# A four-layer hybrid on one core: new ranks for the written-out order, and slot counts in tiles of 96, 112, 104 and 128 rows

## The chip, the core and the metric

The kernel runs on one core of one Trainium2 chip. The metric is the device time of one execution in microseconds (us); the median over runs is what two kernels are compared by. The engines are named as in the profile: PE is the matrix engine (PEld its weight loads), DVE the vector engine, ACT the scalar engine, POOL the engine that also issues indirect DMAs, SP the queue that issues most plain DMAs.

## What is computed

The input x is 16 sequences of 256 tokens with 128 features. Four layers follow each other, each as x = x + layer(layernorm(x)):

```python
x = x + attn_a(layernorm(x))   # softmax over an axis that the einsum then sums out: it comes to x @ (w_v, w_out)
x = x + ffn(layernorm(x))      # 8 experts, each token goes to its best 2, weights by softmax of the two
x = x + attn_b(layernorm(x))   # a selective scan with 16 states per feature, along 256 tokens
x = x + ffn(layernorm(x))      # the same experts again
```

The experts have 128 inputs, 512 hidden units with relu and 128 outputs, all in float32.

## The kernel before, in words

**Blocks and sets.** The 4096 tokens lie in 8 blocks of 512 tokens (2 sequences). For the first expert layer the blocks are grouped into the sets `FIRST = ([0], [1], [2, 3], [4, 5], [6, 7])`, for the second into `SECOND = ([0, 1], [2, 3], [4, 5], [6], [7])`. In a set, each of the 8 experts has a fixed number of slots. `SLOTS` gives that number by layer and by the number of blocks in the set: 192 for one block and 330 for two in the first layer, 216 for one and 384 for two in the second. `divided` cuts the slots into equal tiles of at most 128 rows: 192 = 2 x 96, 330 = 3 x 110, 216 = 2 x 108, 384 = 3 x 128. If an expert draws more tokens than it has slots, a flag is set, and at the end a general kernel computes everything again.

**The stages of one block.** `attention` loads the block (`xT`), transposes it to token rows (`x`), and adds the first layer. `gate` normalises (`xn`), transposes (`xnT`) and multiplies by the gate matrix (`lg`). `route` picks two experts per token and numbers the slots (`to`, `of`), scales the rows (`row`) and scatters them with 8 indirect DMAs per block on POOL into `slots` in DRAM. `experts` takes one expert of a set after the other: a plain DMA on SP fetches its slots (`xs`), PE transposes them, a copy moves them to SBUF (`xsT`), PE makes the hidden units (`ps_b`, relu into `h` on ACT or DVE) and the outputs (`ps_y`, copied into `yT`), PE transposes back, a copy (`yr`) and a plain DMA write `ys` in DRAM. `collect` gathers a block's two results per token with 8 indirect DMAs on POOL (`yy`) and adds them to `x` on POOL or DVE. `mixer` is the selective scan: for each of 8 pairs of states ACT makes `decay` and `th`, PE broadcasts B and C (`ps_B`, `ps_C`, from `pieces` and `sel`), and DVE makes a product on `ps_B`, a scan into `w`, a product on `ps_C` and a product into `th`; two such `th` are added on POOL or DVE and PE sums the result into `ps_s`. At the end `sos` is transposed and added to `x`. `finish` gathers the second expert layer, transposes and stores (`out_T`).

**Who sets the order.** The program is first written down as a list of jobs (`Plan.job`); nothing is emitted then. Each job has one or more ways (engine, duration, call): copies, relus, products of two tensors and row scalings can go to either of two engines. Durations come from the functions `cost` (DVE, ACT, POOL) and `matmul` (PE). `Plan.order` decodes one rank per job from the string `ORDER` and plays the list through (`Plan.forward`): at each step it takes the ready job and engine with the earliest start, and of equal ones the best rank. The result fixes, for each engine, the order of its instructions, which engine does a job that has a choice, and which buffer a tile gets. On the chip each engine then works through its own list in that order, and an instruction that waits holds back all that stand behind it on its engine. So a rank or a duration in the table changes the order and the choice of engine, and no arithmetic.

In a mixer, the pairs are summed like this (`ADD` is 2, `NS` is 16):

```python
            group.append(th)
            if len(group) > 1:
                product(group[0], group[0], th, ALU.add)
            if len(group) == ADD:
                for k in range(2):
                    matmul(so, wsh_s, group[0][:, k, :], False, n + k == NS - 1)
                group = []
```

In the profile, nearly every instruction carries line 710 (the helper that makes the calls); scatters carry line 807 and gathers line 821. The tile names are what tells instructions apart.

Of the kernel before, what the change touches and what calls it, by code (L numbers as in the profile page):

```python
# [40 lines left out]
XN, ROW, XS, XT, H, YT, DEPTH = 4, 3, 4, 3, 4, 3, 3  # L41

ORDER = (
    "c-oy;3zS?{m92a3_kHWtzxw}AcS6!hI-~;z$O;57;6V8Q2_u0S5d^_uSc)<WMU9}iM3yW-9GO9x!6gH;R9KFnMgszpL;?f?f"
    "k*<R^Xq@t@4Y*x(n)u9Rdv$gbywAU_uY5jJ?HGR&pu3!7%XbbZAPKv1@3dL7-PWr9y>~ce89&%(C@K%Jo9!(hVu?i`7ck&TU"
    "=}!eF%Vl)_8eOGlzoV+GCP40*uyj))&`!j{^V`L0}L96gZ<4gs;O)2b>A*3(6>rA1qHftKE)g1PD&+d4C53zj>tYtuRmST4)"
    "&WZ=i;-Wdt8&k}Jkz4frZfW0dx>2F9<qDP7bBq>YMzaZlQu8;l;?+ePSH#x<oKoEc04YdQ9_z#2UcR8YkQZ@_JKUIwrXpCBw"
    "y%n$|z+H*Fet87`^C*_nH1fcC_oYqiEa5-i%s&Llw`v@46X#t7>ItB=v6B`tD>z8D<E*H}0f-#>loAIJY14hsV+|<5QxV>F6"
    ">MACb|KehA*xQaiirRK`r;~{cLjneDt0Nf|kEoo*U@p9_j!i#dWsezvrR+sxshv)zuWsGhFh-7pml~U+|6RMg#e{BnBi1OJ8"
    "{AtKz1A~GTIhQXQRn%ke_1+;3-()<bWZJRR6xkpvtH^UoJyCT1TFBd-vKZw{l=N5^8I7n;k;oMd;@Ct0ds)?$Q&UmPXz}F6#"  # L50
    "dW9?-*SWOvxor10@uUMTT|4)h($^?t#9+p%<8@UwC4u_H&;{uTgXsAMiMbl@4dSA0RXZ4ACKM^vhG!qIZ3nF^_^|>`d-Tn&K"
    "wyzk<LlLQRB1Sh~zY_bopU;AF}%AS(s#+{Wm8iwK;{49U2`nGz1AY|+UEUrmJ%G;LyF9NZ`WH88wyQ>luGWVmKT3OV<!#{EW"
    "z!NIr5>A!W@A}UR$AWI|yFk+BEncN=R!(&QNPwlz&?wY>(L5$Xj@WkfMZ5@g#l8cWfdX#yell3CZhJqETdv4Sl?uKS~-)v})"
    "*4Vd22ckBKk|8VVy=0BLVS=}uE1S@ZYfgCSgm>u8<lgqPqc<;kc?rNJurWMKMhvbR2qEm+|2UcJKs<96Vvpuj0d3D4Ol{~jD"
    "cbd9cbIWM858=Cz7YhCRBII%{;(YO>*0hKYgrutqLc+%P%RBi3%*?jzD0>I3<3Efd@<bwI+I<3KauaD-H2gE37^e)@TEs7Rl"
    "mCTe(M@e{Hq2=o>!CxJnq#en9mpN*lS+&Iw2j!+`ts4{f2PVMHH#yYYq^BZsi=|-|t8(JfC6;{iqKJpA{YQK>8{db}Y7%1%m"
    "$WPD1#pR5Rju3=MF*JyEdPx|=W?&I655)808;G9f7ezWWA3XfwvOg@aHMUvd&5l5TnkS>p^$u;L$4aYP5jbo}#ADG_H0DKuj"
    "u!Z7tjkurLfov96nM^nzTX@8{Q$937vRW0C-5uOb^Oj3%l#B4<#!j~c5E#e_fwC;J+RCpwK|NPft1JPleU~<FVRNIdf6eaz_"
    "Nv0P>Z+A!CEICH}&6*u~1??PyUf7eg8@uY%b;<r%k|>f-k1T$sZg1Me)YxXVdWNeW?%8tuHdp{3#ogBbYA;w0bivzZvubm=S"
    ";u|tWYNdXxF6B#=HHK)3%~O5?RK;+SsOX+qgTI%sagY#bZ33c{lh?fXeo(UeK9XlQ!l>}&R7jB33OpT{afUf*+^D_6L!6*c<"  # L60
    "h7L9m@!!-^s_fy|QfmDvDt?3h}Vp{*$OLDcCS%nsc8svmPfsu)&;TDFcKF;EU}a@<8*34~xXDg|A}%sHpKTeo9dE`>kiXNE!"
    "2}Rao~0CdHr>Vh5vv;!0oyH0!d8k45OvgXmyL7+J<Yl^FG(U|O>XL3Z^p+mWlK0Gj2vl>bFE98-Xh<|d<ttXm_ycw_46$d*="
    "N{H*TW<G$1MvHzy|X*oCAKl|_DUET4E2{EZ~6~SV(+hdkJ2eiw&E}+CZo)u}D7<-j8X)h}#*5`2TRY(d%ak`I(om3YX7XQ;-"
    "82r-(aOFxjFT(DFH3&d<{WUmyg<*(gK;*T8E51PH6`c5O%$++arQY0k=N}_YL3^ZMXC|Hk8Tkp7kug{EMoc)KVA>SNEd*jOR"
    "9YC!pixRCZz|TuC8>TjE2Sd2j>|k}_jex`*77FX%xVN5;iP64HL+aT94Q(>1jRGe9_6W#Uzmtbw}b7x^s&|tS_9HVKCt5A<r"
    ";K3#2~{Q$LJJ~Hs`_xjttq@*ZSwWyjf2SC@AZj@tRoMK)SD!2#kI>vgzGf`??{<_J?ayD>|GN-@g6sACYC`O>cGby6Yag{&{"
    "i}+$XP#SP|(-qF~Kw%fXLgv}ls@Vcf(y{7%z2MX{bU?!9o?c~7re&u%04nm5av&iTz*iXBTg#+qYc$6S5>Z_diGZg@Lf6Z@l"
    ")wW4G;Y_;oS5sUq}{^J@BankP?#tvB!n0-i|(&S41wf@8QeqzI@v|6^xKn>E_@SbQwN(5yWll87$l4ZQ+dV~^R$DnXlPzYRo"
    ")nh#23O4sr7AdIyNKVav-OU8V&iXsz8B^JL-v%twpAwQ=Qp|pL-T}0+fY4v3M`J_Ct2}NOAeM^U#$*H;)v^arT5v56Py~LZy"
    "KtG#Z#A8=wV{w6{Aq2UK4;F$;&&I4XD{lhb2fGEE&R*a#-{EVssn+QktixhOrgXABzgXo6auRe$x$=KXq4BsUH~Xp{8b1kln"  # L70
    "N+6lChLhmik8mt@M}Y;tMZR#K=n$X_u5IpFss8+P{mW+v!LiI0f_TD5d!MEHHWJ{fMhI2>AeM8WT~lFC&MDJMTtfyM<#FVQG"
    "6lvYlzEg5Xy?ijwILJC0%|7jEaAdM4HQ9Ul^>ZtxO2d*7_vQ`_~SaB^+CfzpN?51RLemBMwz*BO@dmSRRDbMiV)Q)90R8v)z"
    "PHZ9pW?~U#))Iqb7HGfO(OYbK0V2jtFoI3HtT9vb*jfliR`xD_|=fpUst#pJqUfuD|?7`1i9dy4PmcQ6C_ua2TI`NL#X@*mg"
    "FRefEuh)`e$Qz<7@yzC)%_k#wz7<VN(?nT?jN!h38#$$@B&A}fNhKD)_V3C>6?W_Km;UG4d2i226s4(^Prc~oj9DzqGETcK8"
    "l1I%Z`po^mmqr`!`l4Z+3U}RBpKnhl}a~$D~2#N!gR!o$meVKHLX;2^h2XY87cFhMkAv)*fxxquK9mk7i_+QICRJ`ksSbxqM"
    "*I8qi^KK9B8|S>`kad*b*wWhc}`O7B-;)d)e~yQKVGI!z@(HG(2T0$>Pb^WShXEOR;`2lv#Y9kQb>_Ogj2i=fq_yU67CeVZr"
    "{@gsGEVbJj_oU$d>DPTCh!;?-g}h~-P|d6M0v5E0K_4$xYQ1gxnot`W$KR~PH@`L`l|7UC;<sTQxWUQ6||poTy22!i!IhKzy"
    "pXQf3l-Gg!A-@Dv~rsY^rO)gVE@UZZmD)VdP0}msHuac5QY{JGYJL#qvpHEjmiedOSa1F&HY|ulVc)O@cHts`I{@eiBjwR(!"
    "_8ix^k!l0(h~&T7vM4e5KVN*DYOK3E+dhbWdb3?O^7)&A1eAW?=7Vz!2K8hi*_g1DL}BPd81oY)3j%rzwa6$#het4-Ihzya7"
    "77H$j6raj9Caxc6jsy)rla2BZ#kLR!ussM?-TivyE_K=-%6eQ%Dy}IKPmF8KGQE(BPY{&sD0aUkypJowK$5&pz3Zxld!;r4b"  # L80
    "i{@8#QJ_IFn*;{VzcdLVpURg@j=$V-dy;p8g9$&<0E*5r}RnW4ssP!0vkwhv!q5M?mqtJQ-&7z$ANdJr>3`CNU5J!(3K065A"
    "i+L-$}&JeEnTAef=kA}-sw&-e>J#HChX&52<yMomPBiDcydpfxkF<esn+mybj<nYg@AEfou;>8oatI$$gl&*zUTVA&_w=>d0"
    ")VuxalN-e>{1?hHd#T<gEY603Sq;ya#Gqh_Mm3NVtcv12paWEAp@N;jl_QKli;?LCjg<s`!{TB$IU6ISyA=LpWVI7x57}ZFu"
    "UyR@ii5A&vj>Y+kR=nMcOp1blceu7K&ZmLJKbnmXE#R8F_*sih9<z#X+;A%6{A{Ez$^$XzqzsgPamGSd;v$zQUxv|TBU}pJO"
    "amc?{~0On8j*%t>`(S5uz_(gF0ig2eO`~@C)l`YfsL7i$mXvUPy{QQMzyN>t{N*$*BV(<B)RH{Zi?qJ-47zZD6A6QTNl6PX5"
    "ISpC}NRp5Pnd{WL_F(JZ&*EA26kJwh%tbQBz`jL{MqK*a1OmW2Y&=;)dCIpY+M<9hn6WW0SGk%=for-_rsND|HXUrYeDY^Wt"
    "uRc9iXm1sqF%8mqwdiz%BgB3yFq0D1xK{)d$SD=|z!!`R#$kn*RmVr&^uNvVT^94rO$#9JszL!=M5ANyV03eex*#vqAJ5%Ny"
    "4jqAju=(&N=4uCL$VU#40LZNbPG?#1NILG;DwkqZqSz2uCi;rN@$1`Lu><|JJbQm8p-oY1<G0KV!2gME%*-8+W+2sVI7iO}V"
    "by#4#`*ZG+D5_>`9E(B_QH4OGPsRbTmB)28Dj{m%J|AhKbS}aVhfpCwQ3T%8MPLEt0_hZ!m=-&iwY`GPJ764^K~`KA)|>;ZT"
    "@}ro$BSFRTs>(OgIUG3@gF-FYys&tR|0K7L5=Q1R;Acpqk2X^1mlt)<4r;#9V#Ar;xBaY8bA8LwH`k|bnD=W9={Cqp~?6mho"  # L90
    "&4_Wy<Nnt3%6`4o`d?Jc7`~W)6IU(A0xWeYE66moHm&C{%Swf1)8>zM4L0V)e(guDC4q`lQj5u0A+aaZ8un3Qd1Ymv1sxdPR"
    "bXpF`2ny4=hvZmZ(jB1TFvQ!y*3d@871G&uZwjyQCLcvtak_0a06QK|H{u2@M=iF$eXLNf~A_>t8mIX5}CBwCXxTAHI}2I<h"
    "`E~}xkx}PS^I0)w{z$;7M(mMgE@bH1*P=z1LhC|cMJ}fL|GOVkadMHZ|Iwe#A`toNgp%6N%#M5OoJ7Xx|oBi^Al<r1{j)cBY"
    "l~?L1sL<2Fxe}N<G+K_!DGWB1<tAJ`9fwY^rJe?ox=L6Hjs_FgT9+F+bp=uascEUaWHugt_1Qsn0t`Y``6H-EgwhO|E(3LFi"
    "Z?4fSLUZ9QdC9!r$s_l{2aE7_!YHqVmIU{%F`z!%!=I%kKZ5%&Cmzc%b~}~q>IM!rb81tqy!K!VUCYqq#7$!!==bhCX=3s;$"
    "%^*;wCa3OO-O9o(ZQ-hqNQio)L;mia^O(WxDCmOmSION~THP!{KuJTjQtx^z2P$M2bgM$Pd4pP-rZqEAXmI7_yZA^bv5zLiv"
    "(<9@0~Uc6m5-C3WfQIGd(iPb1aJH#rlw)TN|RU9cU3796-NOrQ-8{Em$WuY$d&)W2z2U6(ZvewlXCrKM0GRTY^=ugp-!=%Y&"
    "Fsu8My`l0<!hGyKW_?@eYMLo3~SMyobTC68?dK%$h)m{3q^-@n)MyH}zA67bsj(WIKz)be3x{NFe<qcAG^{A`%9Fy8f&&*3R"
# [1408 lines left out]
```

## Time and profile before

| what | value |
|---|---|
| median of 9 runs | 724.24 us (721.89 to 728.17) |
| the profiled execution, its own time | 726.89 us |
| its span on the core | 725.2 us |
| PE busy | 626.5 us (86%) |
| DVE busy | 554.1 us (76%) |
| ACT busy | 487.5 us (67%) |
| POOL busy | 414.0 us (57%) |
| mean granted TensorE clock | 0.915 |

The shares are means over stages of different kind: the beginning, in which the first blocks are loaded and gated, the long middle, in which mixers of some blocks run beside experts of others, and the end, in which only experts are left. The span is the time between the first and the last instruction in the trace; the execution's own time is 1.7 us longer.

### The profile page before, as it was taken

Reading aid. Unit: us, or ns where it says so; the run is one execution under the profiler, and the core shown is the slowest. Engines: PE = TensorE matmul, PEld = TensorE weight load, DVE = VectorE, ACT = ScalarE, POOL = GpSimd, SP = SyncE. Lnnn points to the kernel's source line nnn. Section 1 sums busy time; section 2 is a strip of 40 time slices with the busy share of each in tenths; the row PEclk is TensorE's granted clock in tenths of the full one; section 3 lists DMA queues with packets and bytes.
Section 4 is the critical chain, followed back from the end, with each engine's and each line's share of the span. In section 5 each row is a group of like instructions: output and inputs, shape, how many; then the busy total and the mean of one; then the engine's idle time right before and its main releaser. Section 6 shows DMA issues by size and latency. Waiting matters only on the chain. (4 is left out here: it accounts for less than half of the span.)

```text
span 725.2 us, 8786 instructions
## 1 busy us (share of the span) xinstructions
PE 626.5 (86%) x2598; PEld 392.1 (54%) x2598; DVE 554.1 (76%) x1038; ACT 487.5 (67%) x996; POOL 414.0 (57%) x490
## 2 busy tenths in 40 slices
PE   5478999799999769899898889787999999999970
...
DVE  4765448999998898899999898998898998740120
...
GB/s 234 327 115 52 94 99 42 73 53 47 88 88 17 1 30 46 123 58 33 31 68 83 56 33 25 55 59 21 51 31 80 156 51 70 86 46 104 98 133 76
DMA packets 76373, 55.05 MB, mean 76 GB/s; under 512 B 8064, under 2 KB 69152, under 8 KB 76320
## 3 DMA queue, kind: packets, MB, share of 16 engines
...
q8 instruction: 22, 0.36, 0.2%
...
q14 instruction: 31, 0.25, 0.1%
...
## 5 line engine op out<-in xcount | busy, mean ns | idle before, releaser
L710 PE MATMUL ps_b<-xsT,w_s 128*128 128x330 f32 (+3 forms) x640 | 212.3, 441 | 15.3 <-ACT h L710 6.8
L710 PE MATMUL ps_y<-h,w_s 128*128 128x330 f32 (+3 forms) x640 | 213.9, 425 | 3.4 <-ACT yT L710 2.2
L821 POOL DMA_INDIRECT yy<-ys,of x128 | 124.6, 973 | 101.3 <-DMA ys<-yr 38.5
L807 POOL DMA_INDIRECT slots<-row,to x128 | 126.4, 987 | 79.3 <-issue 22.2
L710 ACT ACTIVATE h<-ps_b 128x384 f32<-128x384 f32 (+2 forms) x234 | 110.1, 475 | 90.0 <-PE ps_b L710 86.4
L710 PEld LDWEIGHTS ps_b<-xsT,w_s 128*128 128x128 f32 x640 | 115.9, 198 | 74.5 <-ACT h L710 24.4
L710 DVE TENSOR_TENSOR_SCAN w<-decay,ps_B 128x1024 f32<-128x1024 f32 x64 | 145.8, 2278 | 0.2
L710 PEld LDWEIGHTS ps_y<-h,w_s 128*128 128x128 f32 x640 | 109.9, 195 | 44.9 <-issue 11.8
L710 ACT ACTIVATE th<-later,lneps,ha_s 128x512 f32<-128x512 f32 x128 | 100.1, 809 | 5.1 <-DVE th L710 2.9
L710 ACT ACTIVATE decay<-delta,nea 128x510 f32<-128x510 f32 x128 | 86.6, 714 | 4.8 <-DVE w L710 3.5
L710 DVE TENSOR_TENSOR ps_B<-du,ps_B 128x1024 f32<-128x1024 f32 x64 | 78.2, 1221 | 13.3 <-PE ps_B L710 13.1
L710 DVE SCALAR_TENSOR_TENSOR ps_C<-th,ps_C 128x1024 f32<-128x1024 f32 x56 | 68.2, 1218 | 7.4 <-PE ps_C L710 7.3
L710 PE MATMUL ps_s<-th,wsh_s 128*128 128x512 f32 x128 | 69.6, 636 | 3.8 <-POOL th L710 3.8
L710 DVE TENSOR_TENSOR th<-ps_C,w 128x1024 f32<-128x1024 f32 x56 | 67.9, 1212 | 0.2
L710 POOL TENSOR_TENSOR th<-th,th 128x1024 f32<-128x1024 f32 x20 | 47.2, 2358 | 29.6 <-DVE th L710 27.2
L710 POOL TENSOR_TENSOR rstd<-var,root 128x8 f32<-128x8 f32 (+1 forms) x20 | 28.2, 1411 | 52.4 <-DVE var L710 49.7
L710 PEld LDWEIGHTS <-sel 96*128 96x128 bf16 x256 | 25.9, 103 | 59.0 <-issue 48.5
L710 PE MATMUL ps_B<-pieces,sel 96*128 96x512 bf16 x128 | 42.0, 402 | 10.3 <-DVE w L710 10.1
L710 PE MATMUL ps_b<-ident,yT 128*110 128x128 f32 (+3 forms) x208 | 43.6, 279 | 3.0 <-ACT h L710 1.5
L710 PE MATMUL ps_b<-ident,xs 110*128 110x110 f32 (+3 forms) x208 | 38.9, 278 | 7.2 <-ACT h L710 3.2
L710 PE MATMUL ps_C<-pieces,sel 96*128 96x512 bf16 x128 | 41.7, 406 | 3.1 <-DVE th L710 2.9
L710 PEld LDWEIGHTS ps_b<-ident,xs 110*128 110x128 f32 (+3 forms) x208 | 26.6, 148 | 26.0 <-ACT h L710 8.5
...
## 6 DMA issues: line engine op xcount, KB each, us to landing
...
slots<-row,to POOLq DMA_INDIRECT x128, 2.3
```

The lines of the kernel that those rows point to most:

```text
L710: return lambda: f(*[real(x) for x in a], **{n: real(x) for n, x in k.items()})
L807: inst = nc.gpsimd.indirect_dma_start(out=real(out), out_offset=bass.IndirectOffsetOnAxis(ap=real(rows), axis=0), in_=real(in_), in_offset ...
L821: nc.gpsimd.indirect_dma_start(out=real(out), out_offset=None, in_=real(in_), in_offset=bass.IndirectOffsetOnAxis(ap=real(rows), axis=0), ...
```

## The change

`SLOTS` becomes `((192, 336, 480, 632), (208, 384, 600, 800))`, so the tiles have 2 x 96, 3 x 112, 2 x 104 and 3 x 128 rows. The durations in `cost` and `matmul` are changed, and `ORDER` is replaced as a whole. In `mixer` a branch is added for the case that a group holds half of the states; with `ADD` at 2 and `NS` at 16 it is not taken.

```diff
-SLOTS = ((192, 330, 480, 632), (216, 384, 600, 800))
+SLOTS = ((192, 336, 480, 632), (208, 384, 600, 800))
 ORDER = (
-    "c-oy;3zS?{m92a3_kHWtzxw}AcS6!hI-~;z$O;57;6V8Q2_u0S5d^_uSc)<WMU9}iM3yW-9GO9x!6gH;R9KFnMgszpL;?f?f"
...
+    "c-pO433Oc5d7gX!yS-)Rz1bwqXqP2fvMmcsmW^$J&1SH%iCGgjEl^Sl3A9O}2MBF)8kVM%l(cZ@Nh#1nfzb3odO`~=C1DQ*h"
...
     def cost(engine, name, views):
         n = max(v.free_size() for v in views)
         if engine == "DVE":
-            t = 0.15 + 0.00208 * n if "scan" in name and n > NE else max(0.2, 0.15 + 0.00104 * n)
-            return t + 0.08 * sum(v.free_size() == 1 for v in views[1:] if n > 1)
+            out, *ins = views
+            ins = [v for v in ins if v.free_size() > 1]
+            fast = name in ("tensor_scalar", "tensor_copy") and not any(
+                v.home.psum or v.dtype != F32 for v in (out, *ins)
+            )
+            t = 0.15 + (0.00208 if "scan" in name and n > NE else 0.00052 if fast else 0.00104) * n
+            return t + 0.07 * sum(v.free_size() == 1 for v in views[1:] if n > 1)
...
     def matmul(out, lhsT, rhs, start=True, stop=True, **order):
         n = rhs.free_size()
-        took = max(0.25 if n <= 16 else 0.42, 0.00178 * n) if rhs.dtype == F32 else max(0.06, 0.00044 * n)
+        took = max(0.23 if n > 16 else 0.2, 0.0017 * n) if rhs.dtype == F32 else max(0.06, 0.00044 * n)
...
             group.append(th)
             if len(group) > 1:
                 product(group[0], group[0], th, ALU.add)
-            if len(group) == ADD:
+            if len(group) == ADD == NS // 2:
+                product(group[0][:, 0, :], group[0][:, 0, :], group[0][:, 1, :], ALU.add)
+                matmul(so, wsh_s, group[0][:, 0, :], False, True)
+            elif len(group) == ADD:
                 for k in range(2):
                     matmul(so, wsh_s, group[0][:, k, :], False, n + k == NS - 1)
                 group = []
```

The number of instructions stays almost the same on every engine. What moves between engines, counted in the two kernels' instruction orders: additions of two `th` go from 12 on DVE and 20 on POOL to 7 and 25; additions of `yy` to `x` from 18 and 14 to 14 and 18; row scalings (`row`) on DVE from 31 to 24; copies into `yr` on DVE from 12 to 24, with as many fewer on ACT.

More of the change, by code (lines that the diff above doesn't have):

```diff
@@ L43 @@
 ORDER = (
-    "c-oy;3zS?{m92a3_kHWtzxw}AcS6!hI-~;z$O;57;6V8Q2_u0S5d^_uSc)<WMU9}iM3yW-9GO9x!6gH;R9KFnMgszpL;?f?f"
[L45 to L98, printed above, removed]
@@ L99 @@
-    "YdmMxAO$n(YeN$ybbOaV6%8^2zS1*j2oGzV{zTp1(Yv#Z&O`qXwp16!"
+    "c-pO433Oc5d7gX!yS-)Rz1bwqXqP2fvMmcsmW^$J&1SH%iCGgjEl^Sl3A9O}2MBF)8kVM%l(cZ@Nh#1nfzb3odO`~=C1DQ*h"
+    "k~(LY>Zh9#x`CgOR_ZEd$<3SVrgbHvIVDOOP+h*efR$N|G)qLzTYMt;RfaP`6IddP0Zukqzo7p2bh!d3p(Z}fF9&A7<#!c@7"
+    "9GGqrZr?aCop5o}?5`zw^r7Ey8CkVtanr|K@#+*GlOBHzl=ib4{uAJwt0oCqB&ATomvCLNx_o0F+V2g8_36-~ymTQi#;Psys"
+    "i^{c-m%&4PEK`_uu67D|J2!I%`Bv2ZV;5ymuQ^Eg*b5la8CkI)1#%|Qd2X%O0S`BDPS_?)s7jZ63n0S+60w+N1hRO9(9O_*A"
+    "<0$2y|h@^2-#@PzO?XlG^^iU=kpTk{_+kvz%qp*rG1<<d!;2dq`8ws3EnMDITK$^h#Nv^dx{Y+zW$H{m%Vnfyt+#SC;&zXb}"
@@ new lines @@
+    "Dmd|^#Cz;faZ4&09^AaBc3<i>Y7xgZ)h7vb7`3VAWRvj?^UjZtxtvGIVNuidtAW~qc9;*_>|WD0YOkppOjOeaberAiK7IBJr"
+    "|ux_<bAis<V#ns@7~$Dk2I1`=8r6YF6EALI){E_q;02~rhAlM*tqMHZV6di*<ST&^iS_#U@*A&0?+omb45mTnIi^i*vnW$5D"
+    "=gq1}rZT6+R>5VT?%(-N^Wi490+Qr2M0#pZURy9}MiH0=j;7>+h`k8f{>d`y2%N3$Df(5B#G5i{U<CQenuo=)5=YB@kso3K{"
+    "0op`F03&G!IZNjU*_2LZt_eC)BSDD)y!AV3YH1|{Oge!>@m@X-`Ym@G;-UwZ+-QU*e@91BZULltYfn9<dQR{_mo)Tl{7byx+"
+    "XagVffwNX{j5yE|tDq>o}_IUs<1f$IoWE!4ewq&BKaq|!FY}`|4Q48|Poco_AzuspM33)s3TpWXI^CrZB5no069ve;!bfWDq"
@@ new lines @@
+    "#k%cCMBTRGKhD`|G?7EjS=Oy9U+F(g*TM_#NtP-2t;s{_2wg>fojk#O>_~KE1+>CW(IhOJQ;TU|EZVt>QBOQ|5f0>GgN;??&"
+    "^7STrP09SKRdOT`>d^LNZzElualHz&Z!#_Sw5ia(f!Oqd{RT@&`$-*jUWr(1+CFto{}8$366^}aClW?gm-i~k0636C6usOI2"
+    "NmkykYRsvyCl>A{g;gF4|<i4^ZGOkxvjz`Src&SGO#|#Wi6=GOq0m;~>wqbB>IE8<R673xaUXd?O-^uW>}jTQ?9At450n(=y"
+    "5M@GY1~;<W1-aj}>HUfb5DGNeg0XZBCf>=r}`CKfac8Dsr~0F2y<`D2AsTuP$yn8V@{=5zk!_bIWKM+#CP&Z1GyWpH<R_j5{"
+    "k6XMTf5;OuFiv$7l3?3Kthtfwz7v7%8WZRxijPR4!Lg0(MpTMewu44@EK>R4CD@aa!LohqPPg+W;xU;+C-R6(y{06E>MAS4s"
@@ new lines @@
+    "Iq&_shsaX;T6J%S>#ECB`|B)nK7Y(yAHK`ZTMnF0A9qiWRYl~t`d?p~VVz{V(~x|i`-3(?y2yKO9gkY<;l*$E43ir2dBV0fS"
+    "0Ah~X@m}0%01C#b{L~?9|1I+;^j|N{^mL^tt;<0>~3K!55IKIwZapOq{xBT{KTWVgc*Zgx-HVRJ}T*&u6I`3<XpPR?vXdN?w"
+    "Yeub-{MG)-<Eyp1!xbhe$Qq&lBzr1;!|CBRkCoZbsz4x9n;iBu!*b!b&~w9tl^`dh(e{npk}SQ&O|6FFYU5<mjGUxZpcgssB"
+    "BZEZb!D*@Us{9#A=R%o>Z_ca1&fWXuug_2{sZQb!^|DG(|g#7Bgw7f?c!`!RTh2~{m<&XC{}#(984%tQl*K{4iu;2b_4(jZ7"
+    "XfH+qyzQ67PLyY#XKe8!ec=~sD{Pp*YdXMe9_wR-uehI_w2#=d?P8~4nIGl)-0*`D$xOOuLBFi8g7EmqniaqoyZo3{)gtP)o"
@@ new lines @@
+    "q6w=BiL%FkP6;%zGm%L;67MP2#<o#yGUFvGMZMc*gCJ}jmx|3nxEg(%2#Ig(*vrC}X|{7@4HsERELlq^^feuHu>JueTOrxt%"
+    "(_m@v3{PURB6l-JlR6j(Rr!)ndVKkBXy0}&tLl18kNc&Y29HJ3JVxy9G_r*Aq>MH#gRmiq!G^dbJJS2YX^%gg`^Q3y5!!5z3"
+    "D?FO%Djy`9S7PpLEh~;YBIg&aMw<5Q{6x)_7y>-O<rhBP^zGh8GE^xpzbL!D^GW(N9$>{z5q0GD_x?cOy+!x?cVycElZnc7R"
+    "C4ePZF;-C>B4K`UG@qbzwj#_CEBdHVvq6X}SK460L3y8l~uf!o8wcSf!{?UwMUouqTf$7X%v*}+7%g?5N{?WJkyy4NI!qBc8"
+    "|yyG<1|BaDX{j`^Cw!7vwDfTDPF=X{N@?m(PdeRwlOnL&{YRyeaX5M?w6BleHm_Tl$`P||+`#(Uw+o|eI!x4a0-4}Nfg1ON7"
@@ new lines @@
+    "A!-bvG3}!)n~Rg>uP~WXD)Pt{)5vFx<dLs;+xa}P^My<8<j6?gG^%Lhr_#2OS(K4w55;_6+-zoj`%y|o2i8`GWJ6qLy2hefw"
+    "?)|O5ZK(v0+lFMs31)(+$Cq81NPW;sUdl@vi;ZU#vc4OrTVL9IFEPYx-MQfuxugWw86BQA5(O<854X9qKp0g9}~)LR2ABmd_"
+    "YveN&5*&fcaf4yYuJm>`I3TJ0NX^8i@e?<R;98n}V{)1msyw%rZd>{^Bs@G*<6+x@|kp`=g~j-EbX31csg=)Vzb8LEDice;r"
+    "xqIw}C5@eUAiz_A_4D14TX7RnLNq#xczX!<NnIYBkk3WZq>5iY$ZIanS2hni7&#WxaJr}uDjNTgRW-zLfriYi{=B%XGeGv+s"
+    "=n~<A*S#7hHUGE4Z%v2ryy#JN?2kH(hqNwYdPqpl6H=rJdRJ6&gs=q#O%9L0@-g6ea|2&Ww?8R#Jl)cVqsEwbM+Fx5!)d|~D"
@@ new lines @@
+    "t<5*o?P*;kPnR#aeU402UEc6{HzCXDD@Kp|w8R2ISJ0QOB}$<zaqNt5KZI~tj<5t48@$Jf%jCehA}plS(eU!4w=8+1Z;&peT"
+    "O-Z!e_gV(Lqe6c-*Ed9w!ET#UtKfpBX3mKg`XHq9$uD8+Ph_)n~cbtTR&?Ev!oi6j<G4{s&#A|^tsQTXFKA?#G%Bw7+cTI$3"
+    "A{~?K78RxyeQHQ6T_ip!mMC`f%(k&L-$5VUM$F{`(RuLaqhv6M?JAv&76c;s`YtfiM+V^yW)kBR;m~#o2bi$df>J31Nx_EB="
+    "<9@;tBVc`i#gvZo_gfAr%EcV`a%-rKnv+t1B0oe#S=0whndvskP(#JL^k)f|KQ_9X@p7vbI-iLhHTCTjb%gul9$(7C6gJPRX"
+    "T*H;M+_bIQI`p={D&PN4{nFMtKuih9$`p^FY>3WT-OHdAt??_{AW1l3HZG3=|@b^(#qub4msMh4kK}D<m6`K8Bg<=*>mssec"
@@ new lines @@
+    "-=W$NXTOh9;5MAe3nj<U5V@K}!u-GG-HF;mdu2oXZYN`LRd6#-|JDUP2VdC1d{lv3tU}}NG2yk7&TT5<f~kaC$fN^J6ZnU3$"
+    "4VS<BuQdXLPRT5s7P;*W&RgEgQoV!kkbPnQ_{fLpV2-ra=#dkN7p5D-b(eUcnSToGQMaB<EV92`rv6R2th?kV?HNhUk&=@7J"
+    "SthK8;Y>2sp$mX=)1jjewknHxR<ELal;Am5(YZkOF)q)mD6%j5z4UCjOes+TFE46x_KDDJ~64d05o*QN<EJM0bfryRd#Oi)3"
+    "7nBehyFizS3M_zj<<(WfKx1)*p~Wh*7#l;^%jNO(DRLISz69!08B6qEMyi$BVq{qwc05Z%r+DycPzvBJ`a|MIy%sNco4Cxq8"
+    "JYMtuqLQNi}F<9tlP(I6svw{XJ#CLL@af03~h9j_%5fQ}#akPgf)2+V|0Sn`y6r$9*T3sd?Sty13KQ*zBmJEOO_Tji+>n_VR"
@@ new lines @@
+    "K4IlO$H~}>)94TrU5h)~hiz%`g{}tj%{CO8U8p3qiH)OW0bkEO$s1P^0cW8XIV!&qD{b?t;HHT)5my&tqDWz4%M>x4c5BRr?"
+    "XRI8FwoHyaV}~UFuQupmQTNm6|R;kj+zf0h|&`!3(&#GuvDKIbeo()7@1fkEtHNAzKl5Ez_s#m6W5@US2JJ8e~P9CI;5ixx1"
+    "7a@$GO!Jt*Ut-CJtYQxhN>V*!Bx9VIISt3j0^U2;qQp?rC8;Oa?j{?_5A`kMCuHyU@DDMEr}9*XK)>xW~@MFNA%pHHG~#GvX"
+    "BdYN0HFzWrV;AQ=ZvXcjJGjo5vy`BBjE0QS;6kn2rY+PiO~q!CwPW^t6>HYIAokAt9K8v<7c@asgq{L|YhZ9;frSA(LKRAKC"
+    "XG!Lg}pyOyDh1zlZD|!g+BGf=#ADD{%ft#u_*`{AgVVppM{33HDaw2v~*im3WgCrX-NN5v=79|@#K!A$jpfUGRM~!!BoMiTK"
@@ new lines @@
+    "HPStlHeLi@u66dh^(cBK%*MEI8nn<qO>^i%TPQ{0#CQ{iXbswa0&a)ZgpL0X0i`#s0J?Zw|2Yser1;`hXA)R|+=(a!Y$X&<e"
+    "f>Oux#&@Xhu{O;ldZdm&=yQqG&Q(daN;!=P}+vXWul~}<9DHUaLWwE4vqxaC!vrI1s|<-XyVVrM~_cUjK_Z_9~G^bc<t!7Q1"
+    "OzZ^TG7dH>PH%b}8DbWMX3FZ~xULtMNlZq3N$o9$hvSn!f5dQ~noxQJ2r_=?}`R(j^`#@p@=-Mi(vCy2MQ-k3v&%DjDiYTS`"
+    "KZoeXO6hDUup{f$ZynjvQTXsjv*!Jly|^o6JNj1Z`Nx-JjUZ=G5>NM%T$@^<O>qg%`zBRzABW_YV4M*8SuU5Xn$wd>?1j;2e"
+    "fLgc1W>G**xa*-|yfG*14vbdMyUKdZ7#(l=v&#=jHSNoOo)1T&pa-^12tZ7gvMUXCqLOC#I$jM_sVRnxuPWD12^|Kh5qzp%)"
```

6 lines of the change are left out of this document (added).

## The prediction

> **What bounds the kernel now.** I read the page first, for its 40 slices. PE is full almost throughout, DVE only in the middle: it comes up in slice 6 and drops out near slice 35, while PE goes on alone.
>
> ```profile
> span 725.2 us, 8786 instructions
> ...
> PE   5478999799999769899898889787999999999970
> ...
> DVE  4765448999998898899999898998898998740120
> ```
>
> So I cut the span where the limit changes and asked for the busy time in five stretches. Their columns are the stretch, its length, then busy us (and instructions) of PE, PEld, DVE, ACT and POOL, the granted clock, the DMA share and GB/s.
>
> ```profile
> 0.00:55.00 55.00, 32.74 (x153) 27.27 (x153) 34.06 (x182) 16.35 (x43) 28.89 (x72) 0.72 0.75 223
> 55.00:127.00 72.00, 66.44 (x368) 54.30 (x368) 40.72 (x172) 38.92 (x98) 41.53 (x58) 0.93 0.26 72
> 127.00:627.00 500.00, 450.91 (x1672) 248.75 (x1671) 458.31 (x618) 392.60 (x764) 303.68 (x312) 0.94 0.20 57
> 627.00:701.00 74.00, 72.33 (x390) 58.69 (x389) 18.64 (x66) 36.68 (x87) 31.39 (x40) 1.00 0.30 86
> 701.00:725.20 24.20, 4.05 (x20) 3.06 (x20) 2.38 (x4) 2.93 (x5) 8.46 (x9) 0.58 0.35 109
> ```
>
> Stage 1 (to 55) is a chain of short steps: nobody is full. Stage 2 (to 127, where DVE begins the first mixer's products) is PE's: 92%. Stage 3 (all eight mixers) is shared: DVE 458.3 of 500, PE 450.9. Stage 4 is PE alone, 98%. Stage 5 is a bare chain. The waits of DVE within stage 3 (total, times, longest) show what its 41.7 idle us are made of: many short waits for PE, whose queue has other matmuls ahead.
>
> ```profile
> DVE ps_B L710 <- PE ps_B L710: 13.1, 15, 2.4
> DVE ps_C L710 <- PE ps_C L710: 7.3, 12, 1.9
> DVE h L710 <- PE ps_b L710: 6.4, 5, 3.2
> ```
>
> Stage 5 in the timeline: the last result goes out at 701.33, the first of its 8 gathers starts 5.09 us later, they run 1.25 us apart, and landing, addition, transposes, copy and store follow.
>
> ```profile
> 701.33 0.80 SPq L710 DMA_DIRECT2D ys<-yr  x1
> ...
> 706.42 0.94 POOL L821 DMA_INDIRECT yy<-ys,of  x1 [4.51 <-DVE x L710]
> ```
>
> (DVE was done at 705.64; the gather waits for the write of `ys`.)
>
> **The widths.** In the timeline, four 216-column float32 matmuls (8 records) take 1.62 us, two take 0.90: 0.36 each, 1.67 ns per column.
>
> ```profile
> 675.30 1.62 PE L710 MATMUL ps_b<-xsT,w_s 128*128 128x216 f32 x8
> ```
>
> 336 for 330: 3 sets x 8 experts x 8 matmuls x 6 columns x 1.67 ns = +1.9 us. 208 for 216: 2 x 8 x 8 x 8 columns = -1.7 us. Net +0.2 on PE; copies and relus change as little (ACT: 440 ns at 330 and 488 at 384 columns, 0.9 ns per column). I take 0. Fewer slots in the second layer could make an expert overflow, and the general kernel would run. I worked the routing out from the reference's inputs: blocks 6 and 7 fill at most 176 and 156 of 208 slots, so that is excluded.
>
> The tiles also change transfers. PE waits for `xs` only 1.0 us from 125 us on, so fetches are hidden, and without that cover a fetch is worth its own wait. The write of 5.09 us in stage 5 is on the path: at best it shrinks with its rows, 8/216 x 5.09 = 0.2; nothing in its row excludes a loss of as much. I take -0.2. The Trainium skill ("DMA: Bandwidth & Descriptors", section "Why a DMA increments its semaphore by 16 and not by 1") says that a DMA uses the largest number of engines up to 16 that divides both sides' slowest dimension. By it 110 rows go over 11 engines and 112 over 16, 108 over 12 and 104 over 13; the last write would have 16 rows per engine for 18, an estimate of -0.6 at most, and the sum below would be 0.4 lower. No row here shows engines by transfer.
>
> **The moved work.** Each term is counted in the instruction orders of both kernels, priced by rows of before: float32 matmuls 1.7 ns per column, transposes 0.125 us (8 in 1.09), the broadcasts 0.22; on DVE by the groups' means.
>
> Stage 1: DVE's work up to the first `to` is 32.0 us before and 32.2 after; `to` no longer stands behind a result of POOL (0.73 us), but a POOL `rstd` (1.67) now stands between the 4th and 5th scatter. Sum about +1 less 1: 0, bounds -2 and +2 (the row's 1.67, rounded up).
>
> Stage 2: PE's work ahead of the first `ps_B` grows from 71.7 to 78.0 us, +6.2. If the mixer's start is set by the chain from set 0's end instead (8 gathers, addition, statistics, transposes, softplus), the delay is that of set 0's end in PE's list: 43.9 to 45.9, +2.0. PE's idle time there (5.6) can take up the difference. I take +4, between them, since both ends lie close.
>
> Stage 3: DVE's work from the first product on `ps_B` to the last addition to `x` falls from 493.1 to 481.6 us: 5 additions of `th` (1.216) -6.1, 3 of `yy` -2.1, 6 `row`, 4 `xn` and 3 `xnT` -4.2, and relus, copies and the rest +0.9 together. My prices exceed the busy time, because neighbours overlap (458.3 for 493.1, a factor 0.93): -10.7. PE's work between the same points falls by 7.4, as what was put ahead of the first mixer is missing here. Both limits fall; DVE's idle 41.7 us stays if waits are as many. I take -10.5, with -7.4 as the other end if PE sets the pace.
>
> The five additions go to POOL at 2.36 us:
>
> ```profile
> L710 POOL TENSOR_TENSOR th<-th,th 128x1024 f32<-128x1024 f32 x20 | 47.2, 2358 | 29.6 <-DVE th L710 27.2
> ...
> L710 DVE TENSOR_TENSOR th<-th,th 128x1024 f32<-128x1024 f32 x12 | 14.6, 1216 | 0.0
> ...
> L710 PE MATMUL ps_s<-th,wsh_s 128*128 128x512 f32 x128 | 69.6, 636 | 3.8 <-POOL th L710 3.8
> ```
>
> POOL has the room (303.7 of 500 busy), and `ps_s` has waited 3.8 us for it in all. Behind a waiting `ps_s` on PE stand experts and the next `ps_B`; I cost it at nothing, and the rival below at what it would be without cover. Do POOL's adds hold DVE up? In stage 1 they do: beside POOL's `batt` additions, DVE steps on 4 elements take 1.20 us, where the same kind takes 0.16 elsewhere.
>
> ```profile
> 15.50 1.20 DVE L710 SCALAR_TENSOR_TENSOR rt<-rt,var 128x4 f32<-128x4 f32 x1
> ```
>
> In stage 3 they do not: the 56 products into `th` lie between 1186 and 1226 ns, whatever POOL does. The skill ("SBUF — State Buffer", the rule that the shared port pair is an exclusive lock) fits both: a DVE step with two SBUF inputs blocks against POOL, and the mixer's steps have one input in PSUM. It would charge only steps such as `z`, `d` and `rt`, at up to 2.36 us each, against this change.
>
> Stage 4: PE's work after the last `sos` goes from 65.8 to 67.1, +1.3. Stage 5: the same 8 gathers and chain, -0.2.
>
> Sum: 0 + 4 - 10.5 + 1.3 - 0.2 = -5.4. The profiled execution took 726.89 us, 1.7 more than its span; it would take 721.5. The median of the runs is 2.65 below that execution, so it goes to **718.8**.
>
> **The rivals.** *POOL holds PE up (slower).* Place: `ps_s` in stage 3, after one of the five moved additions. If POOL stands in a run of four gathers, the addition comes 4 x 1.25 us late and takes 1.1 longer: 6.1 us, with PE's list and then DVE behind it. All five cost 31, three cost 18: 718.8 + 18 = 737. It decides from one such stall (then 725). For it: POOL's busy time in stage 3 grows by about 12 us. Against: 3.8 us for 20 such adds so far. Three stalls at once are unlikely; one or two give 725 to 731. Chance 0.24.
>
> *Waits shrink too.* The old table priced a 192-column matmul at 0.42 us, where 1.67 ns per column make 0.32, and a 216-column one at 0.42 for 0.36, so the old order placed PE's work later than it runs. If a third of DVE's 41.7 idle us goes, the time is 705. For it: the waits for `ps_B` and `ps_C`, 20.4 us, are of this kind. Against: the widths 330 and 384 were priced within 7%, and fill most of stage 3. Chance 0.18.
>
> *Nothing comes of it.* DVE's idle time grows by what it sheds, because ACT (392.6 of 500) or PE sets the pace: 718.8 + 5.4 = 724. Chance 0.18.
>
> **The numbers.** About 0.3% (2.2 us) is what can be told from no change. The forecast has 0.40. Faster: 0.40 + 0.18 = 0.58; same, 722.1 to 726.4: 0.18; slower: 0.24. Downward the range takes in the lower bounds of stages 1 and 2 (-4) and over half of the third of the waits (-8): 707. Upward, the other bounds (2 + 2.2 + 3.1) give 726, two stalls alone 731: 731. Left out are the full third of the waits and the triple stall, under 0.2 together.
>
> **What would show it.** Right: the first `ps_B` product near 131, the last mixer's end about 6 us earlier than now, DVE busy in stage 3 near 448 with 42 idle, and the last `ys` write near 696. Wrong: PE or PEld waiting for POOL `th` by more than 10 us; DVE's idle time in stage 3 above 47 or below 35; the first mixer later than 135.

## The result, and the profile after

The changed kernel takes 737.53 us in the median of 10 runs (735.96 to 739.74) against 724.31 for the kernel before on the same chip: a ratio of 1.018, interval 1.0157 to 1.0204. The forecast was 718.8, with 731 as its upper end. The profiled execution of the new kernel took 734.86 us with a span of 733.1; that of before was 2.6 us above its median and this one is 2.7 below its own, so of the 13 us between the medians the two profiles show 8. Where the other 5 lie is taken up under stage 3 below.

The page first: busy times by slice look like before, only longer at both ends. DVE comes up later and drops out later.

```profile
PE   4567999899998779988669899978999999999970
DVE  3664465789999989997899999999889988641210
```

The same five stages, cut where their limits change in this kernel (columns as before: length, busy us and instructions of PE, PEld, DVE, ACT, POOL, then clock, DMA share and GB/s):

```profile
0.00:55.00 55.00, 30.34 (x134) 25.52 (x135) 30.74 (x184) 17.16 (x45) 25.31 (x70) 0.72 0.74 223
55.00:139.60 84.60, 77.16 (x428) 62.81 (x427) 47.59 (x185) 41.22 (x105) 56.70 (x79) 0.92 0.27 78
139.60:633.00 493.40, 442.09 (x1622) 242.59 (x1621) 451.52 (x596) 390.58 (x752) 309.94 (x300) 0.94 0.20 54
633.00:710.00 77.00, 75.22 (x412) 59.98 (x410) 22.46 (x76) 35.01 (x81) 34.98 (x42) 1.00 0.37 105
710.00:733.10 23.10, 1.74 (x8) 1.14 (x8) 2.77 (x4) 1.27 (x3) 7.62 (x8) 0.59 0.18 54
```

| stage | before | after | difference | forecast |
|---|---|---|---|---|
| 1 and 2, to the first product on `ps_B` | 127.0 | 139.6 | +12.6 | +4 |
| 3, the mixers | 500.0 | 493.4 | -6.6 | -10.5 |
| 4, PE alone | 74.0 | 77.0 | +3.0 | +1.3 |
| 5, the last chain | 24.2 | 23.1 | -1.1 | -0.2 |

The loss is made before the first mixer begins. The windows from 0 to its first product show with what:

```profile
0.00:127.27 127.27, 99.45 (x521) 81.65 (x521) 75.05 (x354) 55.52 (x142) 70.43 (x130) 0.84 0.47 137
0.00:139.58 139.58, 107.47 (x560) 88.31 (x561) 78.31 (x368) 58.37 (x150) 82.01 (x148) 0.84 0.46 135
```

PE has 8.0 us more work behind it (107.47 for 99.45), and 4.3 us more idle time besides (32.1 for 27.8). The timeline of PE shows where it begins: set 0's first transposes of `xs` come 4.4 us later (before, then after). The line above each shows the transposes of `xT` that stand ahead of them. The last two lines of after are for the clock: two matmuls of 192 columns (four records) take 1.65 us at 62 and 0.81 at 69.

```profile
53.32 0.66 PE L710 MATMUL ps_b<-ident,xT 128*128 128x128 f32 x4 [0.32 <-DVE rank L710]
54.66 0.38 PE L710 MATMUL ps_b<-ident,xs 96*128 96x96 f32 x2 [0.68 <-ACT x L710]
57.72 0.66 PE L710 MATMUL ps_b<-ident,xT 128*128 128x128 f32 x4 [1.66 <-DVE rank L710]
59.05 0.58 PE L710 MATMUL ps_b<-ident,xs 96*128 96x96 f32 x2 [0.68 <-ACT x L710]
62.14 1.65 PE L710 MATMUL ps_b<-xsT,w_s 128*128 128x192 f32 x4 [0.52 <-DVE xsT L710]
69.37 0.81 PE L710 MATMUL ps_b<-xsT,w_s 128*128 128x192 f32 x4
```

Up to these transposes PE has the same work behind it (32.4 us before, 32.1 after), so what grew there is waiting. The first fetch of `xs` is issued 1.6 us later (50.59 for 48.98), because POOL makes an `rstd` of 1.68 us between the 4th and 5th scatter, and in PE's list the transposes of `xT` stand ahead and wait 1.66 us for DVE's `rank`, where it was 0.32.

From the transposes to the first product, PE's work is what grew (before, then after):

```profile
54.66:127.27 72.61, 67.05 (x370) 54.57 (x370) 41.33 (x175) 39.18 (x99) 41.76 (x59) 0.93 0.26 72
59.05:139.58 80.53, 75.42 (x409) 61.42 (x410) 44.02 (x168) 40.62 (x104) 53.31 (x73) 0.92 0.28 79
```

This stretch is 7.9 us longer, with 8.4 us more work for PE; its idle time there is 5.1 us, where it was 5.6. Part of it is work of set 1, which comes later in the old order: up to POOL's `rstd` for block 0 (below) PE makes 212 records of 192 columns, where it was 186.

Set 0's first gather comes 7.8 us later (96.09 before):

```profile
103.91 0.99 POOL L826 DMA_INDIRECT yy<-ys,of  x1 [1.79 <-issue]
```

From that gather to the first product on `ps_B` it is 31.2 us before and 35.7 after. All of the difference lies ahead of POOL's `rstd` for block 0: it is at 122.48, 18.6 us behind the first gather, where it was 14.1 before (110.19), and from there to the first product it is 17.1 us in both. On DVE, the additions of `yy` to block 0's `x` stand behind a copy of `yT` that waits 1.52 us for PE, and the statistics behind a copy of `yr` that waits 2.04 us:

```profile
116.80 0.36 DVE L710 COPY yT<-ps_y 128x192 f32<-128x192 f32 x1 [1.52 <-PE ps_y L710]
117.08 1.41 DVE L710 TENSOR_TENSOR x<-x,yy 128x512 f32<-128x512 f32 x2
121.43 0.42 DVE L710 COPY yr<-ps_b 96x256 f32<-96x256 f32 x1 [2.04 <-ACT h L710]
122.48 1.04 POOL L710 TENSOR_TENSOR rstd<-var,root 128x4 f32<-128x4 f32 x1 [1.35 <-DVE var L710]
139.58 1.21 DVE L710 TENSOR_TENSOR ps_B<-du,ps_B 128x1024 f32<-128x1024 f32 x1
```

### The profile page after: what moved, and what is told of

Read it like the earlier page. It is cut to its first block, busy times and chain, and to the rows that moved or that the text cites. A ratio compares the mean times of both kernels' runs of the same rounds, so it can differ in the third digit from the quotient of the medians.

```text
span 733.1 us, 8791 instructions
## 1 busy us (share of the span) xinstructions
PE 626.5 (85%) x2598; PEld 392.0 (53%) x2598; DVE 555.1 (76%) x1041; ACT 485.2 (66%) x984; POOL 434.6 (59%) x497
## 5 line engine op out<-in xcount | busy, mean ns | idle before, releaser
L710 PE MATMUL ps_b<-xsT,w_s 128*128 128x336 f32 (+3 forms) x640 | 212.1, 443 | 9.6 <-ACT h L710 3.3
L710 PE MATMUL ps_y<-h,w_s 128*128 128x336 f32 (+3 forms) x640 | 213.9, 425 | 2.4 <-ACT h L710 1.9
L812 POOL DMA_INDIRECT slots<-row,to x128 | 129.0, 1008 | 71.1 <-issue 26.6
L710 ACT ACTIVATE h<-ps_b 128x384 f32<-128x384 f32 (+2 forms) x231 | 109.2, 476 | 93.5 <-PE ps_b L710 89.5
L710 POOL TENSOR_TENSOR th<-th,th 128x1024 f32<-128x1024 f32 x25 | 59.3, 2372 | 33.1 <-DVE th L710 19.4
L710 PE MATMUL ps_s<-th,wsh_s 128*128 128x512 f32 x128 | 71.1, 650 | 4.6 <-POOL th L710 4.4
L710 PE MATMUL ps_C<-pieces,sel 96*128 96x512 bf16 x128 | 41.9, 395 | 10.9 <-DVE th L710 10.6
L710 ACT COPY yT<-ps_y 128x336 f32<-128x336 f32 (+3 forms) x71 | 29.1, 410 | 25.7 <-PE ps_y L710 24.4
L710 PE MATMUL ps_b<-ident,xs 112*128 112x112 f32 (+3 forms) x208 | 38.6, 277 | 6.0 <-DVE x L710 2.4
L710 PE MATMUL ps_b<-ident,yT 128*112 128x128 f32 (+3 forms) x208 | 41.7, 281 | 1.3 <-ACT yT L710 0.4
```

Source lines behind the costliest of these rows:

```text
L710: return lambda: f(*[real(x) for x in a], **{n: real(x) for n, x in k.items()})
L812: inst = nc.gpsimd.indirect_dma_start(out=real(out), out_offset=bass.IndirectOffsetOnAxis(ap=real(rows), axis=0), in_=real(in_), in_offset ...
```

## The experiments

All kernels below carry the order of the work as a fixed list, so that one thing can be changed while the rest of the order stays (a plan made anew would move everything). Where jobs are moved or two lists are joined, the buffers of later tiles change too:

```diff
     def order(self):
-        end, start, way, buffer = self.made = self.forward(rank)
...
+        # jobs in sequence, engine by job, buffer by tile: read from ORDER
```

"Old" and "new" order are the lists that the kernels before and after come to. "First product" is block 0's first product on `ps_B`; it is read from one execution each. Profiles of the same order differ: in four with the old order and 192 slots it is at 127.27 to 129.91, in four with the new list up to it at 138.24 to 139.58. So the 12.3 us of the pair above is the widest that these profiles allow, and near 10 their mean. Verdicts rest on the ratios, each against runs of the kernel before on the same chip. **Theory "start"**: the order of the work ahead of the first mixer costs the time, by PE's pace. **Rivals**: the widths; a loss spread over the whole order; POOL (its added scatters, or its additions of `th`).

**Widths and order apart.**

```diff
-SLOTS = ((192, 330, 480, 632), (216, 384, 600, 800))
+SLOTS = ((192, 336, 480, 632), (208, 384, 600, 800))   # with the old order; and the reverse with the new one
```

Old order, new widths: 

> The order, engines and buffers of the kernel before, written out as a fixed list, with the new SLOTS (336 and 208) and nothing else of the change. Theory 'start' (the loss is in the order of the work ahead of the first mixer, the widths cost nothing): 724 us, within 2 of the kernel before, first product on ps_B near 127. Rival 'widths' (tiles of 112 and 104 rows cost PE or transfers what was lost): up to 737; a loss of over 4 us would be charged to the widths.

Measured: 722.97 us, ratio 0.9953 (0.992 to 0.9985), first product at 129.91.

New order, old widths: 

> The order, engines and buffers of the kernel after, written out as a fixed list, with the old SLOTS (330 and 216). Theory 'start': 737 us as the kernel after, 13 over the kernel before, first product on ps_B near 139. Rival 'widths': back to 724, or by as much as the widths' share.

Measured: 740.39 us, ratio 1.0216 (1.0181 to 1.0252), first product at 138.24. So the widths lose nothing; they may bring up to 0.8%. The order alone costs 15 us (740.39 less 725.35).

**The start alone.** The first jobs come from the new list, all others follow in the old one's sequence:

```diff
+first = [x for x in new if planned[x] < T]      # T = 62 or 128 us
+order = first + [x for x in old if x not in first]
```

> Old widths. The first 490 jobs in the new order (what it plans before 62 us: gates and routes of the first blocks, the first fetches of set 0), then the rest in the order of the kernel before. Theory 'start', with the loss already made when set 0's first expert begins (4.4 us later on PE in the new kernel): first product on ps_B 4 to 8 us later than before, total 728 to 732. Theory 'start', with the loss made later, among the experts of sets 0 and 1: within 2 us of 724. Rival 'spread' (the new order loses a little everywhere): 725 to 726.

Measured: 727.60 us, ratio 1.004 (1.0007 to 1.0074); first transposes of `xs` at 59.89, first gather at 100.04, first product at 131.27. The time lies between the two forms of the theory.

> Old widths. The first 1061 jobs in the new order (all that it plans before 128 us, to just behind the first mixer's first product), then the rest in the order of the kernel before. Theory 'start': the first product on ps_B near 139, 12 us late, and the rest takes as long as before or somewhat longer, since the two lists do not join smoothly: 736 to 745. Rival 'spread': 727, since only a sixth of the order is new. Rival 'middle' (the loss is made beside the mixers): 724.

Measured: 739.96 us, ratio 1.020 (1.0148 to 1.0253), first product at 139.06.

The first quarter of the new list is enough for the whole loss: from its first product to the end this kernel takes 598.8 us (span 737.9), and the kernel before 597.9. The part planned before 62 us makes the first product 1.4 to 4.0 us late, by which profile of the old order one takes; the jobs planned between 62 and 128 us make the other 8.

**Is it PE's pace?** Take work from PE in sets 0 and 1 in both orders:

```diff
-SLOTS = ((192, 336, 480, 632), (208, 384, 600, 800))
+SLOTS = ((160, 336, 480, 632), (208, 384, 600, 800))
```

Old order: 

> The same kernel as s160_old_order (160 slots for one block in the first layer, old order), since the chip of that comparison took 809 us for the kernel before as well. Theory 'PE sets the start of the new order, and the old order has slack there': ratio to the kernel before 0.991 to 0.995 (719 to 722 where that takes 725), the first product on ps_B 1 to 4 us earlier than with 192 slots. Rival 'the chain over POOL and DVE sets the start in both': the same gain in both orders, 0 to 2 us.

Measured: 726.43 us, ratio 1.0019 (0.9981 to 1.0056); with 192 slots it was 0.9953.

New order: 

> The same kernel as s160_new_order (160 slots for one block in the first layer, new order). Theory 'PE sets the start of the new order': the first product on ps_B 6 to 9 us earlier than with 192 slots, near 132, ratio to the kernel before 1.005 to 1.010 (with 192: 1.018). Rival 'the chain over POOL and DVE sets the start': 0 to 2 us earlier, ratio 1.016 to 1.018.

Measured: 732.64 us, ratio 1.009 (1.0059 to 1.0121); with 192 it was 1.018. The two first products, old order and new:

```profile
125.11 1.21 DVE L763 TENSOR_TENSOR ps_B<-du,ps_B 128x1024 f32<-128x1024 f32 x1
133.10 1.21 DVE L763 TENSOR_TENSOR ps_B<-du,ps_B 128x1024 f32<-128x1024 f32 x1
```

In the new order 6.8 us less work for PE bring the first product 6.5 us forward (139.58 to 133.10) and the total down by 0.9%, 6.5 us. In the old order the total does not fall. Its first product is earlier too (129.91 with 192 slots and the new widths, 127.27 in the kernel before), but the stretch from there to the last mixer's addition to `x` was longer in the profiled execution (507.0 us for 502.1 and 505.4). So the expectation for the old order (0.991 to 0.995) was missed. The rival with POOL and DVE falls for the new order. In the old one the first product is 2.2 to 4.8 us earlier, which does not quite exclude it; its total does not hang on its start, and the new one's does. Narrower slots also shorten copies and relus: ahead of the new order's first product ACT loses 1.5 us of work and DVE 0.5, PE 6.4. The test takes most from PE, but it does not separate PE from these.

**Is the added work the cause?** The 14 jobs of set [2, 3]'s first expert that the new list puts ahead of the first product go behind it:

```diff
+move = [x for x in head if x belongs to expert 0 of set [2, 3] and is no fetch]
+order = (head without move) + [first product] + move + rest
```

> The same kernel as n_expert0_behind_mixer0. Theory 'filler': the first product stays at 139 within 1 us, ratio to the kernel before 1.018 to 1.026. Rival 'cause': the first product near 136, ratio 1.012 to 1.014.

Measured: 743.65 us, ratio 1.0249 (1.0199 to 1.0299), first product at 138.72.

It came 0.9 us earlier, within what profiles of one order differ by, with 3.8 us of PE's work (by the counted prices) gone from ahead of it. From block 0's `rstd` to the first product it takes 17.4 us then, with PE busy for 14.5, and 17.1 with PE busy for 16.9 in the new kernel. So this work stood in gaps that PE has there while block 0's own chain goes on. The same with the 16 row scalings and 13 scatters of blocks 4 and 5:

> The new order and the new widths; the 16 row scalings and 13 scatters of blocks 4 and 5 that stand ahead of block 0's first product on ps_B are put just behind it. Theory 'PE sets the start': the first product stays at 138 to 140. Rival 'POOL's queue sets it' (13 scatters more stand there than before): it comes 3 us earlier or more. The total grows in both, by 5 to 20 us, as set [4, 5] is fetched later.

Measured: 755.31 us, ratio 1.0415 (1.035 to 1.0479), and the first product did not move (139.86), so these scatters are not the cause.

**The additions of `th`.**

```diff
+way[x] = way_before[x]      # for the 15 additions of th that had changed engine
```

> The same kernel as n_adds_as_before. Theory 'the additions bring the middle its gain': the stretch from first product to last addition to x gets 4 to 6 us longer than in the new kernel, ratio to the kernel before 1.023 to 1.026. Rival 'POOL holds PE up at ps_s': ratio below 1.014. Third way: DVE has as much idle time around them, and the ratio stays at 1.016 to 1.020.

Measured: 741.97 us, ratio 1.0225 (1.0176 to 1.0275). The ratio is 0.0045 above that of the new kernel, some 3 us, with intervals that overlap, so a gain from the move to POOL is likely and not shown. From the first product to the last addition to `x` it was 505.3 us for 499.0, but the same stretch takes 504.2 in the new order with the old widths, where the additions are on POOL. POOL does not hold PE up: giving additions back did not make the kernel faster.

The kernels with 160 slots, with the first expert's work moved and with the additions given back were first run on a chip on which the kernel before took 809.11 us; there the ratios were 0.9977 and 1.0029 (160 slots, old and new order), 1.0076 and 1.0035. In the profile of one, PE's weight loads wait 89.5 us for nothing that the profile shows (35.7 in the profile of the same kernel on another chip). The orders lie closer together there than on the other chips; that such stalls cover the difference is likely, and no run shows it.

**An order that holds under longer durations.** If the new durations are too short for what stands ahead of the first mixer, an order searched under longer ones should win:

> An order of my own, as a fixed list, with the new widths: ranks changed step by step from those of the kernel before, each step kept if the mean of two played-through ends fell: one with the old durations, one with the new durations in which PE's jobs under 0.4 us take 1.15 times as long and PE runs at half speed until 60 us. Theory 'prices' (the new order lost because its durations are too short for PE ahead of the first mixer): an order that holds under both prices keeps its start, first product on ps_B near 125, and has a shorter middle; 712 to 720 us, ratio 0.983 to 0.993. Rival 'any new order loses on the chip what it gains on paper': 723 to 735, first product after 130.

Measured: 729.91 us, ratio 1.0063 (1.003 to 1.0097), first product at 128.59, and 503.9 us from there to the last addition to `x`. Half of the theory fell: the start stayed near the old one's, but the middle did not get shorter beyond the spread, and the stage behind it got longer. The time lies in the rival's range. And with 160 slots:

> The order of v_searched_both_prices with 160 slots for one block in the first layer (6.8 us less work for PE in sets 0 and 1). If PE sets its start: 3 to 6 us less than with 192. If it has slack there, as the old order: within 2 us of it.

Measured: 726.78 us, ratio 1.0007 (0.9972 to 1.0043), 3.1 us less: the lower edge of the first case, with intervals that overlap.

**The widths one by one, and a wider step** (old order):

> The old order as a fixed list with 336 for 330 slots, 216 kept. Theory 'by stage' (the gain of the widths comes from 216 to 208 columns in stage 4, where PE is full; 336 is covered by the middle): 724 to 727, ratio 0.999 to 1.003. Rival '112 rows move faster than 110': 722 to 723, ratio 0.995 to 0.997.

Measured: ratio 1.0001 (0.9969 to 1.0033).

> The old order as a fixed list with 208 for 216 slots in the second layer, 330 kept. Theory 'by stage': 1.7 us less for PE in stage 4, a ratio of 0.996 to 0.998. Rival 'widths bring nothing': 0.999 to 1.002.

Measured: ratio 0.9993 (0.9959 to 1.0026), which does not tell the two apart.

```diff
-SLOTS = ((192, 330, 480, 632), (216, 384, 600, 800))
+SLOTS = ((192, 336, 480, 632), (192, 384, 600, 800))
```

> The old order as a fixed list with 336 slots for 330 in the first layer and 192 slots (2 x 96 rows) for 216 in the second, which these inputs fill to 176 at most. The 128 matmuls of the two last sets get 24 columns narrower: 5.1 us less for PE at 1.67 ns per column, in stage 4, where it is full. Theory 'by stage': 4 to 6 us less than with 216 (719 to 721, ratio 0.992 to 0.994 or below), the first gather of the last eight near 703. Rival 'widths cost and bring nothing' (the prediction's term): 0.998 to 1.002.

Measured: 720.47 us, ratio 0.9935 (0.9909 to 0.9962). It is faster than both kernels. From the last mixer's addition to `x` to the first of the last gathers it takes 70.2 us (632.01 to 702.25) where the kernel with 336 and 216 takes 73.6 (629.47 to 703.05). So 3.3 of the 5.1 us that PE saves there arrive.

## Why the prediction was wrong, step by step

**Widths: 0.** It stands within what the runs can tell: each alone changes nothing beyond 0.4%, both together bring 0.2 to 0.8% in one comparison. By the Trainium skill's rule ("DMA: Bandwidth & Descriptors", section "Why a DMA increments its semaphore by 16 and not by 1") a transfer of 112 rows goes over 16 engines and one of 110 over 11. Here 336 for 330 slots gave a ratio of 1.0001, so no gain in the kernel's time is seen; PE had waited only 1.0 us for `xs` from 125 us on, and no run shows how long a transfer of 110 rows takes.

**Stages 1 and 2: +4. This step failed; it measured +12.6 in this pair of profiles, and 8 to 12 over all of them.** Two terms of the sum were wrong. Stage 1 stood at 0 with bounds of 2: set 0's first transposes of `xs` came 4.4 us late, without more work for PE. The sum had seen POOL's `rstd` between two scatters (it shows as 1.6 us in the fetch), but set it off against a gain elsewhere; it had nothing for the place of these transposes in PE's list, behind others that wait for DVE's `rank`.

Stage 2 was put at +4, between the delay of the chain (+2.0) and that of PE's list (+6.2), because PE's idle time of 5.6 us was to take up the difference. It took up nothing: from the transposes to the first product PE's work grew by 8.4 us, its idle time went from 5.6 to 5.1, and the stretch grew by 7.9. The delay of set 0's end, read from the list as 2.0 us, was 7.8. So the lower of the two bounds was no bound, and the upper was too low.

The experiments order the causes. The list up to the first mixer holds all of the loss (739.96 us with the old order behind it). Less work in sets 0 and 1 brings the first product forward in step (6.5 us for 6.8 us of PE's work). The first expert of set [2, 3] and the added scatters are filler. The stretches say where the time goes: 4.4 us ahead of set 0's first transposes, 3.4 from there to the first gather, 4.5 from the gather to block 0's `rstd`, and none behind it. In the third of these stretches, block 0's additions and statistics stand on DVE behind copies that wait for PE, so PE's delay is handed on through DVE's list. Which jobs would have to go back for the chain to be as fast as before stays open: no run moves set 1's work alone.

I also had no term for durations that the new table understates. It prices a 192-column matmul at 0.33 us (0.0017 x 192), where the old table had 0.42; the lines above show two of them in 0.81 us at full clock and in 1.65 while the clock is 0.50, until 69 us. That the shorter price made the new order's start late is argued and not shown: the order searched under longer ones kept its start, but did not win.

**Stage 3: -10.5. In this pair -6.6; over all profiles a gain is not shown.** DVE's busy time fell from 458.3 to 451.5, by 6.8 for the 10.7 forecast, and its idle time is 41.9 us, as forecast 42. The five additions came as costed (14.6 to 8.6 us, -6.0). The mis-sized term is the rest, "+0.9": copies and relus that went to DVE (`xsT`, `yr` and `h` +6.4, `yT` -2.1) alone made +4.3. The waits for `ps_B`, `ps_C` and `h` shrank (13.1, 7.3 and 6.4 before), but others came in their place:

```profile
DVE ps_B L710 <- PE ps_B L710: 8.9, 14, 2.0
DVE ps_C L710 <- PE ps_C L710: 5.6, 11, 1.3
DVE h L710 <- PE ps_b L710: 6.1, 6, 2.1
DVE xsT L710 <- PE ps_b L710: 4.3, 2, 3.9
DVE lg L710 <- PE ps_b L710: 2.5, 1, 2.5
```

Another execution shows less. The kernel with the new order and the old widths has the same engines for the same jobs. From the first product to the last addition to `x` (the new kernel, then this one; 505.41 us with DVE busy for 460.10 in the kernel before) DVE is busy for 5.1 us more, and the stretch is 5.1 us longer:

```profile
139.58:638.62 499.04, 447.69 (x1643) 245.68 (x1642) 453.24 (x598) 392.26 (x755) 310.79 (x300) 0.94 0.20 54
138.24:642.40 504.16, 452.55 (x1643) 249.86 (x1642) 458.35 (x597) 391.19 (x755) 310.37 (x300) 0.92 0.19 53
```

In four profiles of the old order the stretch takes 500.9 to 505.4 us. So the new kernel's profile is one with a short middle, and the 5 us that it lies short of the difference of the medians are of this size.

**Stage 4: +1.3 became +3.0; stage 5: -0.2 became -1.1.** PE stayed full in stage 4 (75.22 of 77.0), with 2.9 us more work for the 1.3 counted. In stage 5 the last write and its first gather are now 3.4 us apart for 5.1:

```profile
710.12 0.83 SPq L710 DMA_DIRECT2D ys<-yr  x1
713.55 0.95 POOL L826 DMA_INDIRECT yy<-ys,of  x1 [5.51 <-DMA ys<-yr]
```

This comes with the order, and not with the rows: with the old widths in the new order it is 3.49 us, with the new widths in the old order 5.34, and with 208 slots alone 4.84. The prediction put the 5.09 us down to the write, but the profile names DVE's addition to `x` as what that gather waited for, and in all profiles of the old order the gather starts within 0.8 us of that addition's end. So no row shows a write of 5 us, and the estimate of -0.6 from the number of engines had no such time to shrink.

**The rivals.** POOL holding PE up is refuted: PE waits 4.4 us for POOL's `th`, where it was 3.8, for 25 additions instead of 20, and giving them back made nothing faster.

```profile
PE ps_s L710 <- POOL th L710: 4.4, 5, 1.8
```

"Waits shrink too" held for the waits named, not for their sum. The Trainium skill ("SBUF — State Buffer", the shared port pair as an exclusive lock) would have charged small DVE steps against the change. Steps that ran 0.35 us or more over the shortest of their kind beside a two-input step of POOL were, from 100 us on, 5 before and 8 after, longer by 6.0 us in all and 7.6. That agrees, and it is not the cause of the late start. In the new order with the old widths there were 7, longer by 12.1 us, which is most of what DVE is busier by in that execution. One of them, a kind of step that takes 0.20 us in the median, lasted through two steps of POOL:

```profile
324.68 4.15 DVE L763 TENSOR_TENSOR oh<-rank,at 128x64 f32<-128x64 f32 x1
325.17 2.36 POOL L763 TENSOR_TENSOR th<-th,th 128x1024 f32<-128x1024 f32 x1
327.47 1.27 POOL L763 TENSOR_TENSOR x<-x,yy 128x512 f32<-128x512 f32 x1
```

The prediction took 2.36 us as the most that one step can lose; this one lost 3.9. It also had no term for such steps in stage 3, where in some executions they take back what DVE sheds.

Of my signs, the first mixer later than 135 was the one that called the forecast wrong, and it did. The chance of 0.24 for slower was given to a mechanism in the middle; no rival looked at the chain ahead of the first mixer, though stage 2 was where I had found the most work added.
